# A two-layer graph network on one core: a new opening of set-up, and a fixed place for each load of A

## The chip, the cores and the metric

The kernel runs on one core of one Trainium2 chip. The metric is the device time of one execution in microseconds (us), as the median of several runs. A core has five engines that matter here: TensorE (PE in the profile, with PEld for its weight loads), VectorE (DVE), ScalarE (ACT), GpSimd (POOL) and SyncE (SP). SP, ACT and POOL also issue the DMA transfers that this text speaks of. Each engine takes its own instructions in their order.

## The reference

The input is x (4096 x 512) and a symmetric 0/1 adjacency matrix A (4096 x 4096). Two layers follow each other, each with a residual and a layer norm. Cut to what matters:

```python
# layer 0: graph attention with 8 heads of 64
feats = einsum('nf,hfo->hno', x, W)
s_self, s_neigh = einsum(feats, a_self), einsum(feats, a_neigh)    # one number per head and node
dense = leaky_relu(s_self[:, :, None] + s_neigh[:, None, :], 0.2) * A
out = softmax(dense) @ feats + b
x = layernorm(x + relu(out))
# layer 1: attention inside 32 graphs of 128 nodes, with A added to the scores
q, k, v = x @ Wq.T + bq, x @ Wk.T + bk, x @ Wv.T + bv
scores = (where(mask, q @ k.T * scale, 0) + 2 * A) * where(mask, 1, -1e6)
x = layernorm(x + (softmax(scores) * mask) @ v)
```

## The kernel before

**Stages.** Set-up (0 to about 160 us) makes the features of layer 0 and all that depends on one node alone. Four passes follow, one for each pair of heads r = 0 to 3. A pass goes over four chunks c of 1024 target nodes, and in each chunk over the 32 tiles j of 128 source nodes, eight at a time in passes 0 to 2 and four at a time in pass 3. Pass 0 also turns A: it loads A, transposes it, and stores the result in DRAM (`at_d`), from which passes 1 to 3 read. Layer 1 runs inside and after pass 3.

**Who orders the work.** PE's instructions stand in the order in which the program writes them. For the other engines and for DMA issues a scheduler chooses the order, except for an instruction that is given to `tc.keep_in_program_order`. A tile pool with n buffers makes the n+1st tile wait until the first is no longer used.

**Set-up.** x is treated in eight blocks k of four tiles u of 128 rows. For each block:

- `load_rows(k)` loads four x tiles (`xt_f`, pool of four). Block 0 is issued on SP, the others on ACT.
- `turn_rows(k)` transposes them on PE, 16 transposes (L650), into four PSUM tiles `ps_set` (pool of three; in block 0 the last goes to a `ps_m` bank), one for each 128 columns c of x. ACT copies each to SBUF as `xT_f` (L653), and sums it on the way into `xs`.
- `features(k, u)` multiplies a tile with W (`w_sb_f`) into `ps_fe` (L722, pool of two): eight instructions, which the profile records as sixteen. W has two more columns a head, W a_self and W a_neigh, so that the scores come out with the features. In block 0 the first three tiles go without them (256 columns in place of 264), and `first_scores` (L746) makes up for them.
- DVE adds b (L733), which frees the `ps_fe` buffer; `exponentials` make the factors that depend on one node (`e_all`, `pu_j`, `d_all`).
- `scaled_features(k, u)` makes what the passes multiply with: ACT writes `fst` (L775), DVE writes a second part of `fst` (L776) and `gst` (L766), and POOL stores both to DRAM as `f_d` and `g_d`.
- `rows_of_exponentials(k)` stores rows of factors, `pu_d`, one block later.

The two score columns of W are made at the start on DVE: for each of the four chunks c of W two multiplies (L634) and two reductions (L635), with a_self and a_neigh spread over all partitions in one `fst` buffer (the pool has three). The transposes of block k+1 stand behind the first product of block k, except for block 1, whose transposes stand behind the third product of block 0.

**Loads of A.** `load_adjacency(c, j)` issues on POOL a load of 1024 x 512 elements of A (`a_b`, converted to 8 bits, pool of three). Such a block holds four tiles j. The first three are issued in set-up; every other is issued by `bring(0, c, j)` at the tile that needs it, and the scheduler moves it up. `bring` transposes two tiles of A at once on PE (L1130), ACT casts them to `at` (L1134, twelve buffers in passes 0 to 2), and POOL stores them (`at_d`, L1135).

**One step of pass 0.** For eight tiles j: DVE makes sixteen `q` (L1386, eight buffers), ACT and DVE the marks (L1395, L1391); PE computes `accf` (L1406, from `at` and `f_s`), transposes A for four coming tiles, computes `acc` (L1426, from `q` and `g_s`), `dens` (L1441, from the marks) and `ae` (L1350, from `at`), and transposes A for four more. SP loads `f_s` and `g_s` (two buffers each) for every four tiles, and `p_row` (two buffers) and `u_row` (one) for every chunk c.

Of the kernel before, what the change touches and what calls it, by code (L numbers as in the profile page):

```python
# [10 lines left out]
F32 = mybir.dt.float32  # L11
# [393 lines left out]
def adjacency_streamed_path(  # L405
# [159 lines left out]
    def sums_to_columns(dst, part):  # L565

        for m in range(FC):
            nc.tensor.matmul(
                dst[:, m : m + 1], part[:, ts(m, P)], pick_col, start=True, stop=True
            )  # L570

    ats = {}
    a_bs = {}
# [12 lines left out]
    with tc.tile_pool(name="setup1", bufs=1, side="right") as one, tc.tile_pool(  # L586
# [28 lines left out]
        a_b2 = staged.tile([P, PR, 2, 2, FP], F32R, name="fst").bitcast(F32)  # L615
        a_b2 = a_b2[:, :2].rearrange("p r u s n -> p (r u s n)").rearrange(
            "p (k h o) -> p k h o", k=2, h=H
        )
        for k, v in enumerate((a_self, a_neigh)):
            nc.sync.dma_start(  # L620
                a_b2[:, k].rearrange("p h o -> p (h o)"), broadcast_rows(v, P, H * FH)
            )
# [7 lines left out]
        load_rows(1)  # L630
        for c in range(FC):
            prod = qp.tile([P, C], F32, name="q").rearrange("p (k h o) -> p k h o", k=2, h=H)
            for k in range(2):
                nc.vector.tensor_mul(prod[:, k], w_sb[:, c, :, :FH], a_b2[:, k])  # L634
                nc.vector.tensor_reduce(w_sb[:, c, :, FH + k], prod[:, k], AX.X, OP.add)  # L635
# [3 lines left out]
        xs = one.tile([P, FC, NB], F32, name="xs")  # L639

        def turn_rows(k):
            xT = xTs[k] = two.tile([P, FC, 4, P], F32, name="xT_f")
            pts = {}

            order = [(u, c) for u in range(4) for c in range(FC)]
            for u, c in order if k == 0 else sorted(order, key=lambda x: x[1]):
                if u == 0:
                    last = k == 0 and c == FC - 1
                    pts[c] = misc([P, 4, P]) if last else pss.tile([P, 4, P], F32, name="ps_set")
                nc.tensor.transpose(pts[c][:, u, :], xts[k][u][:, ts(c, P)], ident)  # L650
            for c in range(FC):
                pt = pts[c]
                nc.scalar.activation(  # L653
                    xT[:, c], pt, AF.Identity, accum_out=xs[:, c, k : k + 1]
                )
# [59 lines left out]
        def features(k, u):  # L715
            pf = psf.tile([P, 2, HB], F32, name="ps_fe")
            pf = pf[:, :, : H * FW // 2].rearrange("p q (h w) -> p q h w", w=FW)
            scored = k > 0 or u == 3
            cols = slice(0, FW if scored else FH)
            for c in range(FC):  # L720
                for q in range(2):
                    nc.tensor.matmul(  # L722
                        pf[:, q, :, cols],
                        tile_j(xTs[k][:, c].rearrange("p u n -> p (u n)"), u),
                        w_sb[:, c, 4 * q : 4 * q + 4, cols],
                        start=(c == 0),
                        stop=(c == FC - 1),
                    )
# [12 lines left out]
        def first_scores():  # L741

            ps = pss.tile([P, 4, H, 2], F32, name="ps_set")
            for u in range(3):
                for c in range(FC):
# [7 lines left out]
                    )  # L753
            for u in range(3):
                exponentials(0, u, ps[:, u].rearrange("p (q h) w -> p q h w", q=2))

        def scaled_features(k, u):
            j, v, i = 4 * k + u, u // 2, u % 2
            fb = sums[k, v][:, i]
            if i == 0:  # L760
# [14 lines left out]
            nc.scalar.activation(fst[:, :, i, 0, :], fr, AF.Copy, scale=-1.0)  # L775
            nc.vector.scalar_tensor_tensor(  # L776
                fst[:, :, i, 1, :],
# [4 lines left out]
                op1=OP.subtract,  # L782
            )
            if i:
                for dst, n, src in (
# [330 lines left out]
    def bring(r, c, j):  # L1116
# [12 lines left out]
        for t in range(CT):  # L1129
            nc.tensor.transpose(pt[:, t, :], pairs[:, t, :], ident_b)  # L1130
        both = pt.rearrange("p t n -> p (t n)").bitcast(FP8).rearrange("p (n k) -> p n k", k=2)
        for k in range(2):
# [192 lines left out]
    def main_pass(r, ae=None, wide=4):  # L1325

        for c in range(NCH):
            p_row = []
            for h in range(2):
                p_row.append(rowp.tile([P, C], F32, name=f"p_row{h}"))  # L1330
                nc.sync.dma_start(p_row[h], broadcast_rows(pu_d[2 * r + h, ts(c, C)], P, C))
            u_row = urowp.tile([P, C], F32, name="u_row")
            for h in range(2):
                nc.sync.dma_start(
                    u_row[h * FH : (h + 1) * FH, :],
                    broadcast_rows(pu_d[H + 2 * r + h, ts(c, C)], FH, C),
                )
# [23 lines left out]
            for j0 in range(0, NT, wide):  # L1361
# [3 lines left out]
                for k in range(j0 // 4, (j0 + wide) // 4):  # L1365
                    f_s[k] = fsp.tile([P, 4, 2, FP], F32R, name="f_s")
                    nc.sync.dma_start(
                        f_s[k].rearrange("p u s n -> p (u s n)").bitcast(F32), f_d[r, k]
                    )
                    g_s[k] = gfp.tile([P, 4, 2, FH], F32, name="g_s")  # L1370
                    nc.sync.dma_start(g_s[k].rearrange("p u h o -> p (u h o)"), g_d[r, k])
                if at_step == 0:
# [178 lines left out]
```

## Time and profile before

| | |
|---|---|
| median of three runs | 2067.01 us (2066.73 to 2069.36) |
| the profiled execution | 2068.04 us, of which the profile's span is 2066.2 us |
| PE busy | 2030.9 us, 98% of the span |
| DVE, ACT, POOL busy | 81%, 75%, 11% |
| set-up, from the first instruction to the first transpose of A | 159.8 us |
| PE's first transpose, PE's first product L722 | 3.91 us, 13.93 us |
| mean share of the DMA engines, 60 to 120 us and 120 to 620 us | 1.04, 1.03 |

The profile is of one execution. Its span runs from the first to the last instruction of the core; the execution's own time has 1.8 us around it. The granted clock of PE is given as a share of full speed. A wait is put down to the work that ended last ahead of it.

### The profile page before, as it was taken

The numbers are of one execution on the slowest core, as the hardware profiler recorded it, in microseconds if no ns is written. First come the engines' busy times: TensorE is split into PE (matmuls) and PEld (weight loads), VectorE is DVE, ScalarE is ACT, GpSimd is POOL, SyncE is SP. The second block draws the span as 40 slices with busy tenths as digits, with TensorE's granted clock in tenths as the row PEclk, the third lists the DMA queues.
The fourth block names the chain that finished last, engine by engine and source line by source line (L and its number), as shares of the span: only waits on it lengthen the run. The fifth ranks groups of instructions, "written<-read, shape, count | busy, mean of one in ns | idle before, by whom it ended". The sixth has DMA issues, their size and how long they took to land.

```text
span 2066.2 us, 38253 instructions
## 1 busy us (share of the span) xinstructions
PE 2030.9 (98%) x15086; PEld 1049.8 (51%) x15086; DVE 1670.1 (81%) x2125; ACT 1540.4 (75%) x1869; POOL 222.9 (11%) x361
## 2 busy tenths in 40 slices
PE   8999999999999999999999999999999999999997
PEld 6885555444445444444445444444454445445443
DVE  5667888888799998798999899998975884896654
ACT  3338888888878899788899899998885666567420
POOL 1223222222100000000000000000210210210111
PEclk9999999999999999999999999999999999999999
DMA  6989999999899999798999899989974773684211
GB/s 195 303 270 248 270 294 263 296 260 297 264 341 335 367 347 350 258 312 293 327 308 338 300 354 329 329 287 360 315 247 150 240 262 128 229 275 167 74 49 43
DMA packets 207371, 551.31 MB, mean 267 GB/s; under 512 B 24780, under 2 KB 65740, under 8 KB 207180
## 3 DMA queue, kind: packets, MB, share of 16 engines
q1 hardware_dynamic: 136716, 418.45, 58.1%
q0 software_dynamic: 62272, 121.91, 23.1%
q10 hardware_dynamic: 8192, 8.39, 1.2%
q8 instruction: 121, 1.98, 0.4%
q14 instruction: 70, 0.57, 0.1%
HBM read 491.79 MB, written 107.22 MB: 290 GB/s over the span
## 4 chain that ended last, share of the span: by engine, by line
PE 84%; DMA 7%; issue 4%; DVE 2%; ACT 1%; POOL 1%; POOLq 0%; ACTq 0%; DVEq 0%; SPq 0%
PE acc L1426 36%; PE accf L1406 20%; PE ps_m L1067 5%; PE ps_fe L722 5%; PE ps_m L995 5%; DMA at_d<-at 5%; PE dens L1441 5%; PE ps_m L1022 1%; DVE q L1386 1%; PE ps_m L1081 1%; DMA xt_f<-in_x_dram 1%; ACT mark L1395 1%; PE ps_m L975 1%; PE ps_m L1130 1%; PE ps_m L924 1%
## 5 line engine op out<-in xcount | busy, mean ns | idle before, releaser
L1386 DVE SCALAR_TENSOR_TENSOR q<-p_row,d_all,at 128x1024 f32<-128x1024 f32 x1024 | 1241.9, 1277 | 159.9 <-PE acc L1426 129.3
L1395 ACT ACTIVATE mark<-q,nb_all 128x1024 fp8e4<-128x1024 f32 x896 | 995.5, 1145 | 181.4 <-DVE q L1386 165.8
L1426 PE MATMUL acc<-q,g_s 128*32 128x512 f32 x8192 | 904.2, 593 | 1.4 <-DVE q L1386 0.4
L1426 PEld LDWEIGHTS acc<-q,g_s 128*32 128x32 f32 x8192 | 264.3, 110 | 595.3 <-issue 533.6
L1406 PE MATMUL accf<-at,f_s 128*128 128x512 f32 x2048 | 496.7, 398 | 1.9 <-issue 1.8
L1406 PEld LDWEIGHTS accf<-at,f_s 128*128 128x128 f32 x2048 | 380.5, 189 | 111.4 <-issue 28.1
L1151 ACT ACTIVATE ck<-ck,neg_half_f 128x1024 f32<-128x1024 f32 x128 | 146.0, 1141 | 21.7 <-DMA ck<-in_adj_dram 21.7
L1152 ACT ACTIVATE ck<-ck,neg_quarter 128x1024 f32<-128x1024 f32 x128 | 146.4, 1143 | 1.7
L1441 PE MATMUL dens<-mark,e_b 128*6 128x512 fp8e4 x2048 | 125.9, 379 | 0.9 <-ACT mark L1395 0.9
L722 PE MATMUL ps_fe<-w_sb_f,xT_f 128*128 128x264 f32 (+1 forms) x512 | 121.3, 394 | 4.6 <-ACT xT_f L653 4.6
L1134 ACT CAST at<-ps_m 128x1024 fp32r<-128x1024 fp8e4 x128 | 120.1, 1026 | 5.5 <-ACT mark L1395 3.0
L1067 PE MATMUL ps_m<-wvT,x1T 128*128 128x512 f32 x256 | 114.2, 594 | 0.0
L995 PE MATMUL ps_m<-x1T,M_sb 128*128 128x512 f32 x256 | 112.9, 595 | 0.0
L722 PEld LDWEIGHTS ps_fe<-w_sb_f,xT_f 128*128 128x128 f32 x512 | 100.7, 200 | 19.1 <-ACT xT_f L653 5.0
L1271 POOL DMA_DIRECT2D hs_d<-hst x12 | 10.7, 893 | 834.4 <-DVE hst L1261 816.1
L1391 DVE TENSOR_SCALAR mark<-q,d_all 128x1024 fp8e4<-128x1024 f32 x128 | 95.7, 748 | 4.8
L1441 PEld LDWEIGHTS <-e_b 128*6 128x6 bf16 x2048 | 55.8, 86 | 78.5 <-issue 36.2
L1135 POOL DMA_DIRECT2D at_d<-at x128 | 69.0, 539 | 178.0 <-ACT at L1134 107.4
L995 PEld LDWEIGHTS ps_m<-x1T,M_sb 128*128 128x128 f32 x256 | 48.0, 190 | 59.3 <-issue 58.4
L1067 PEld LDWEIGHTS ps_m<-wvT,x1T 128*128 128x128 f32 x256 | 47.6, 190 | 56.4 <-issue 55.1
L1075 DVE TENSOR_TENSOR v_t<-ps_m,bv_row 128x512 f32<-128x512 f32 x32 | 21.7, 683 | 60.5 <-PE ps_m L1067 60.5
L1002 ACT ACTIVATE zT<-ps_m,zb 128x512 f32<-128x512 f32 x32 | 21.8, 680 | 61.1 <-PE ps_m L995 61.1
(185 smaller groups left out, 1084.2 us busy)
## 6 DMA issues: line engine op xcount, KB each, us to landing
at<-at_d SPq DMA_DIRECT2D x384, 512.0 KB, 6.0
f_s<-f_d SPq DMA_DIRECT2D x128, 512.0 KB, 7.5
at_d<-at POOLq DMA_DIRECT2D x128, 512.0 KB, 14.9
ck<-in_adj_dram SPq DMA_DIRECT2D x128, 512.0 KB, 5.4
g_s<-g_d SPq DMA_DIRECT2D x128, 256.0 KB, 5.7
f_d<-fst POOLq DMA_DIRECT2D x16, 1024.0 KB, 7.2
a_b<-in_adj_dram POOLq DMA_DIRECT2D x32, 512.0 KB, 16.3
p_row<-pu_d SPq DMA_DIRECT2D x32, 512.0 KB, 6.7
```

Of the source, the lines that this page charges most:

```text
L722: nc.tensor.matmul(pf[:, q, :, cols], tile_j(xTs[k][:, c].rearrange("p u n -> p (u n)"), u), w_sb[:, c, 4 * q : 4 * q + 4, cols], start=(c ...
L995: nc.tensor.matmul(pz, L1["M"][:, f, ts(c, P)], x1T[:, f, :], start=(f == 0), stop=(f == FC - 1),)
L1067: nc.tensor.matmul(pv, x1T[:, f, ts(u, P)], L1["wvT"][:, f, :], start=(f == 0), stop=(f == FC - 1),)
L1134: nc.scalar.copy(at, both[:, :, k])
L1151: tc.keep_in_program_order(nc.scalar.activation(ck, ck, AF.Square, bias=neg_half))
L1152: nc.scalar.activation(ck, ck, AF.Abs, bias=neg_quarter, accum_out=binp[:, k : k + 1])
L1386: nc.vector.scalar_tensor_tensor(q, p_row[h], d_j, ats[r, c, j].bitcast(F32), op0=OP.max, op1=OP.mult)
L1391: nc.vector.tensor_scalar(mark, q, d_j, None, op0=OP.is_gt, saturate=False)
L1395: nc.scalar.activation(mark, q, AF.Sigmoid, bias=nb_all[:, j, hh : hh + 1], scale=BIG, saturate=False,)
L1406: nc.tensor.matmul(accf[:, s, :], f_s[j // 4][:, j % 4, w, :], ats[r, c, j][:, ts(s, HB)], start=(j == 0 and w == 0), stop=(j == NT - 1 an ...
L1426: nc.tensor.matmul(acc[o : o + 32, s, :], g_s[j // 4][:, j % 4, h, o % FH : o % FH + 32], qs[j, h][:, ts(s, HB)], start=(j == 0), stop=(j ...
L1441: nc.tensor.matmul(dens[lo : lo + 6, :], e_b[:, j, 2 * r + h, :], marks[j, h][:, ts(s, HB)], start=(j == 0), stop=(j == NT - 1),)
```

## The change

It has two parts.

In set-up, SP issues the first two x tiles, then the second half of W, a_self, a_neigh (now in an `fst` buffer each), the other two x tiles, b, and all later x tiles; ACT issues only the first half of W, and then runs a one-column activation at once. Block 0 is turned in two halves: two tiles are transposed and copied, the product of tile 0 and the first half of that of tile 1 follow, then the other two tiles are transposed. Ahead of the first and of the second x tile PE transposes the unit matrix, nine times and twice (`keep_warm`), into a `ps_fe` buffer that no one reads. None of block 0's four tiles takes its scores with its features now; `first_scores` covers all four and comes behind tile 3, as do block 1's transposes. The score columns of W's second half are made behind the first two products. Several instructions are pinned to the program's order.

In pass 0, `bring` issues the load of the block three places up right behind the transposes of a block's second half. The loads of `p_row` and `u_row` of the first two chunks and of `f_s` and `g_s` of the first sixteen tiles are pinned.

```diff
+    def in_order(pinned, ins):
+        if pinned:
+            tc.keep_in_program_order(ins)
...
-        def load_rows(k):
-            xts[k] = []
-            for u in range(4):
+        def load_rows(k, us=range(4)):
+            xts.setdefault(k, [])
+            for u in us:
                 xt = xtp.tile([P, F], F32, name="xt_f")
-                queue = nc.scalar if k else nc.sync
-                queue.dma_start(xt, x[ts(4 * k + u, P), :])
+                nc.sync.dma_start(xt, x[ts(4 * k + u, P), :])
...
-        load_rows(0)
+        load_rows(0, (0, 1))
...
-            nc.scalar.dma_start(
+            queue = nc.scalar if c < FC // 2 else nc.sync
+            queue.dma_start(
                 w_sb[:, c, :, :FH], W[:, ts(c, P), :].rearrange("h p o -> p h o")
             )
...
+        nc.scalar.activation(neg_quarter, neg_quarter, AF.Identity)
...
+            nc.sync.dma_start(a_s[k], broadcast_rows(v, P, H * FH))
+        load_rows(0, (2, 3))
         b_row = one.tile([P, H * FH], F32, name="b_row")
         nc.sync.dma_start(b_row, broadcast_rows(b, P, H * FH))
+        load_rows(1)
...
+        def score_columns(c, pinned=True):
...
+        for c in range(FC // 2):
+            score_columns(c, False)
...
+            def keep_warm(n):
+                pw = psf.tile([P, 2, HB], F32, name="ps_fe")
+                for i in range(n):
+                    nc.tensor.transpose(pw[:, 0, :P], ident, ident)
+
+            order = [(u, c) for u in us for c in range(FC)]
             for u, c in order if k == 0 else sorted(order, key=lambda x: x[1]):
...
+                if (k, c) == (0, 0) and u < 2:
+                    keep_warm((9, 2)[u])
+                nc.tensor.transpose(turned[c][:, u, :], xts[k][u][:, ts(c, P)], ident)
...
-            scored = k > 0 or u == 3
+            scored = k > 0
...
+                if (k, u, c) == (0, 1, 1):
+                    turn_rows(0, (2, 3))
...
-            for u in range(3):
+            for u in range(4):
                 for c in range(FC):
                     nc.tensor.matmul(
                         ps[:, u],
...
-        turn_rows(0)
+        turn_rows(0, (0, 1))
         for k in range(NB):
             for u in range(4):
                 features(k, u)
-                if u == (0 if k else 2) and k + 1 < NB:
+                if k == 0 and u < 2:
+                    score_columns(FC // 2 + u)
+                if u == (0 if k else 3) and k + 1 < NB:
                     turn_rows(k + 1)
...
-                if u == 2 and k == 0:
+                if u == 3 and k == 0:
                     first_scores()
...
+        ahead = c * NT + j + 10
+        if j % 4 == 2 and ahead < NCH * NT:
+            tc.keep_in_program_order(load_adjacency(ahead // NT, ahead % NT))
...
+                in_order(
+                    r == 0 and c < 2,
+                    nc.sync.dma_start(p_row[h], broadcast_rows(pu_d[2 * r + h, ts(c, C)], P, C)),
+                )
...
+                    in_order(r == 0 and c == 0 and j0 < 16, ins)
```

In the changed kernel L650 becomes L674, L653 becomes L677, L722 becomes L749, L733 becomes L762, L775 becomes L804, L634 and L635 become L638 and L642, L746 becomes L775, and L1130 becomes L1162.

More of the change, by code (lines that the diff above doesn't have):

```diff
@@ L611, in adjacency_streamed_path @@
         for c in range(FC):
-            nc.scalar.dma_start(
+            queue = nc.scalar if c < FC // 2 else nc.sync
+            queue.dma_start(
                 w_sb[:, c, :, :FH], W[:, ts(c, P), :].rearrange("h p o -> p h o")
             )
[L615 to L618, printed above, removed]
+        nc.scalar.activation(neg_quarter, neg_quarter, AF.Identity)
+        a_s = [staged.tile([P, PR, 2, 2, FP], F32R, name="fst").bitcast(F32) for _ in range(2)]
+        a_s = [a.rearrange("p r u s n -> p (r u s n)")[:, : H * FH] for a in a_s]
         for k, v in enumerate((a_self, a_neigh)):
-            nc.sync.dma_start(
-                a_b2[:, k].rearrange("p h o -> p (h o)"), broadcast_rows(v, P, H * FH)
-            )
+            nc.sync.dma_start(a_s[k], broadcast_rows(v, P, H * FH))
+        load_rows(0, (2, 3))
         b_row = one.tile([P, H * FH], F32, name="b_row")
         nc.sync.dma_start(b_row, broadcast_rows(b, P, H * FH))
+        load_rows(1)
         b_col = one.tile([P, PR], F32, name="b_col")
@@ L629, in adjacency_streamed_path @@
         )
-        load_rows(1)
-        for c in range(FC):
+        def score_columns(c, pinned=True):
             prod = qp.tile([P, C], F32, name="q").rearrange("p (k h o) -> p k h o", k=2, h=H)
             for k in range(2):
-                nc.vector.tensor_mul(prod[:, k], w_sb[:, c, :, :FH], a_b2[:, k])
-                nc.vector.tensor_reduce(w_sb[:, c, :, FH + k], prod[:, k], AX.X, OP.add)
+                ins = nc.vector.tensor_mul(
+                    prod[:, k], w_sb[:, c, :, :FH], a_s[k].rearrange("p (h o) -> p h o", h=H)
+                )
+                in_order(pinned, ins)
+                ins = nc.vector.tensor_reduce(
+                    w_sb[:, c, :, FH + k], prod[:, k], AX.X, OP.add
+                )
+                in_order(pinned, ins)
+        for c in range(FC // 2):
+            score_columns(c, False)
         powers = one.tile([P, 5, H], F32, name="powers")
@@ L638, in adjacency_streamed_path, with turn_rows @@
             nc.vector.memset(powers[:, i, :], v)
[L639 to L645, printed above, removed]
+        xs = one.tile([P, FC, NB + 1], F32, name="xs")
+        turned = {}
+        def turn_rows(k, us=range(4)):
+            if us[0] == 0:
+                xTs[k] = two.tile([P, FC, 4, P], F32, name="xT_f")
+                turned.clear()
+            xT, n = xTs[k], slice(us[0], us[-1] + 1)
+            for c in range(FC):
+                if us[0] == 0:
+                    last = k == 0 and c == FC - 1
+                    turned[c] = misc([P, 4, P]) if last else pss.tile([P, 4, P], F32, name="ps_set")
+            def keep_warm(n):
[3 more added lines that the diff above has]
+            order = [(u, c) for u in us for c in range(FC)]
             for u, c in order if k == 0 else sorted(order, key=lambda x: x[1]):
[L647 to L650, printed above, removed]
+                if (k, c) == (0, 0) and u < 2:
+                    keep_warm((9, 2)[u])
+                nc.tensor.transpose(turned[c][:, u, :], xts[k][u][:, ts(c, P)], ident)
+            at = NB if us[0] else k
             for c in range(FC):
-                pt = pts[c]
                 nc.scalar.activation(
-                    xT[:, c], pt, AF.Identity, accum_out=xs[:, c, k : k + 1]
+                    xT[:, c, n],
+                    turned[c][:, n],
+                    AF.Identity,
+                    accum_out=xs[:, c, at : at + 1],
                 )
@@ L753, in first_scores @@
                     )
-            for u in range(3):
+            for u in range(4):
                 exponentials(0, u, ps[:, u].rearrange("p (q h) w -> p q h w", q=2))
@@ L775, in scaled_features @@
             nc.scalar.activation(fst[:, :, i, 0, :], fr, AF.Copy, scale=-1.0)
-            nc.vector.scalar_tensor_tensor(
+            ins = nc.vector.scalar_tensor_tensor(
                 fst[:, :, i, 1, :],
@@ L783, in scaled_features @@
             )
+            in_order(k == 0, ins)
             if i:
@@ L1330, in main_pass @@
                 p_row.append(rowp.tile([P, C], F32, name=f"p_row{h}"))
-                nc.sync.dma_start(p_row[h], broadcast_rows(pu_d[2 * r + h, ts(c, C)], P, C))
+                in_order(
+                    r == 0 and c < 2,
+                    nc.sync.dma_start(p_row[h], broadcast_rows(pu_d[2 * r + h, ts(c, C)], P, C)),
+                )
             u_row = urowp.tile([P, C], F32, name="u_row")
             for h in range(2):
-                nc.sync.dma_start(
-                    u_row[h * FH : (h + 1) * FH, :],
-                    broadcast_rows(pu_d[H + 2 * r + h, ts(c, C)], FH, C),
+                in_order(
+                    r == 0 and c < 2,
+                    nc.sync.dma_start(
+                        u_row[h * FH : (h + 1) * FH, :],
+                        broadcast_rows(pu_d[H + 2 * r + h, ts(c, C)], FH, C),
+                    ),
                 )
@@ L1366, in main_pass @@
                     f_s[k] = fsp.tile([P, 4, 2, FP], F32R, name="f_s")
-                    nc.sync.dma_start(
+                    ins = nc.sync.dma_start(
                         f_s[k].rearrange("p u s n -> p (u s n)").bitcast(F32), f_d[r, k]
                     )
+                    in_order(r == 0 and c == 0 and j0 < 16, ins)
                     g_s[k] = gfp.tile([P, 4, 2, FH], F32, name="g_s")
-                    nc.sync.dma_start(g_s[k].rearrange("p u h o -> p (u h o)"), g_d[r, k])
+                    ins = nc.sync.dma_start(
+                        g_s[k].rearrange("p u h o -> p (u h o)"), g_d[r, k]
+                    )
+                    in_order(r == 0 and c == 0 and j0 < 16, ins)
                 if at_step == 0:
```

## The prediction

> **What bounds the kernel now.** I read the page's part 1 first, then the list of what TensorE (PE) waited for, then the chain of waits over the first 45 us, then the table by stretches. The page says who is full:
>
> ```profile
> PE 2030.9 (98%) x15086; PEld 1049.8 (51%) x15086; DVE 1670.1 (81%) x2125; ACT 1540.4 (75%) x1869; POOL 222.9 (11%) x361
> PE   8999999999999999999999999999999999999997
> ```
>
> PE is busy in 2030.9 of 2066.2 us; only the first and last slices fall below 9. So a change can gain PE's idle time where it acts, PE work done at a low clock, or PE instructions that it removes. The idle time, from PE's waits:
>
> ```profile
> PE ps_set L650 <- DMA xt_f<-in_x_dram: 6.4, 4, 3.9
> PE ps_fe L722 <- ACT xT_f L653: 4.6, 1, 4.6
> PE ps_m L1130 <- ACT at L1134: 2.0, 2, 1.2
> PE ps_set L695 <- ACT pu_j L671: 1.3, 1, 1.3
> PE dens L1441 <- ACT mark L1395: 0.9, 2, 0.7
> ```
>
> (engine, waiting line, releaser: us, times, longest.) The first two, 11.0 us, lie in set-up: 9.8 at the opening and 1.24 at 92.7 us, where block 5's x came late. The other three lie at the end of set-up and in pass 0. No transpose of A (L1130) waits for its load. The opening, as the chain (start, us, what):
>
> ```profile
> 0.73 3.05 DMA xt_f<-in_x_dram
> 3.78 0.02 issue
> 3.80 8.09 DMA w_sb_f<-in_L_gnn_W_dram
> 11.89 0.00 issue
> 11.89 1.28 ACT L653
> 13.17 0.01 issue
> 13.19 0.70 ACT xT_f L653 x2
> 13.88 0.04 issue
> 13.93 12.03 PE ps_fe L722 x48
> 25.95 1.87 PE ps_set L650 x16
> 27.83 3.06 PE ps_set L746 x24
> 30.88 8.75 PE ps_fe L722 x32
> 39.63 1.93 PE ps_set L650 x16
> ```
>
> PE had all of block 0's transposes done by 9.3 us. ACT, which must copy them out, was still issuing: four loads of W, then four of block 1's x at 7.39 to 11.86, each behind an earlier transfer. Then it loaded its table (1.28), and the first product started at 13.93. The landmark is 39.63, block 2's transposes: before and after, the same products precede it and from there the two PE orders agree.
>
> **What the Trainium skill says.** "TensorE: Matmul & The Clock Gate", Part 1, says that PE's clock is halved by default, and that free-running windows of about 3.4 us decide. The trace agrees: these stretches (PE busy, clock, DMA share, GB/s) hold scores, then dense products, half speed, then full again.
>
> ```profile
> 27.05:30.46 3.41, 3.41 (x29) 1.00 0.98 316
> 30.46:33.87 3.41, 3.41 (x10) 0.50 0.67 237
> 33.87:37.28 3.41, 3.41 (x17) 1.00 0.01 2
> ```
>
> "ScalarE: Activation LUTs", What ACT_TABLE_LOAD costs, gives 1283 ns; here 1.28 us. "DMA: Bandwidth & Descriptors", Issuing engines are not separate DMA queues: a second issuing engine saves issue time alone, so moving x from ACT to SP adds no bandwidth; what it can free is ACT. The same page's Specifications want 512 bytes a piece for full rate; W's pieces are 256 bytes (4096 packets for 1 MB), so I count W double.
>
> **The change, part by part.**
>
> *Opening loads.* SP now issues x tiles 0, 1, W chunks 2, 3, a_self, a_neigh, x 2, 3, b, x of block 1; ACT issues W 0, 1 and loads its table near 3 us. x 1 should land as before, 5.7. W's first landing took 6.3 us after issue, so W 0 at 7.0 to 7.4. PE's first product therefore starts at 7.2 instead of 13.93: 6.7 earlier. ACT's first half-copy, near 6.5, is not last there.
>
> *What is late next.* DVE. Before, a_self landed at 9.07 behind 1 MB of x and part of W; now it is behind 0.5 MB of x and most of W. Counted double where it is W, that is 2.75 MB against about 2.4 at some 0.37 MB/us: 10.2. From there DVE works 8 multiplies and reduces for W 0, 1 (8 x 0.64 = 5.1), a small cast (0.2), and the bias add L762 (0.7): 16.2. In the built order ACT has the scaled copy L804 of tile 0 *ahead of* the copies of x tiles 2 and 3, so those wait for DVE: 16.3 + 0.63 + 0.5 = 17.5. Tile 2's product starts there. PE's own path comes close: tile 0 from 7.2 (cold until about 10, then 2.1) to 12.1; half of tile 1, 1.7; 8 transposes, 0.9 (x 2 and 3 are issued once W 0 has landed, whose semaphore they share in the built program, so they land near 7.2 + 5.1 = 12.3, in time); the other half, 1.7: 16.5. So PE idles 1.0, and half of what the early start wins is given to DVE.
>
> *From there to the landmark.* Warm rates are 223 ns per 264-column record (3.57 for 16), scaled to 216 for 256 columns; scores 122 ns. Tiles 2 and 3: 2 x 3.46. Transposes of block 1: 1.9. Scores, now for four tiles: 32 x 0.122 = 3.9 (8 records more than the 24, +1.0, less 0.1 for a narrower tile 3). Tile (1,0): 3.57. A cold window after the scores, as before: 3.4 us at half, 1.7. Sum 17.5 + 6.92 + 1.9 + 3.9 + 3.57 + 1.7 = 35.5. Gain 39.63 - 35.5 = **4.1**.
>
> *Unit transposes.* 11 x 0.21 cold = 2.3 us of PE, issued from 1.5 us on while PE has no data. Cover: the wait for x 0 (3.88) and x 1 (5.7). Without it they cost up to 2.3. Their gain is at most the cold loss before 10 us, 1.4; behind DVE it is worth 0. I take 0, range -0.5 to +1.4.
>
> *x on SP; p_row, u_row, f_s, g_s behind it.* In 60 to 95 us, p_row and u_row landings took 12.7 to 13.8 us and x up to 11.7; block 5's x was 1.24 late. In the new SP order all 28 x loads precede them, so they go out at about 106 to 115, still 35 us ahead of pass 0. I take the 1.24 as gained; bounds 0 (congestion stays, the shares at 60 to 110 being 1.04 and more) and 1.24. f_s/g_s of cycle 0 have the same cover. Removing 28 issues of about 0.35 to 1.3 us from ACT is worth nothing more: PE bounds that stage.
>
> *Pinned SP order in pass 0.* With T for the first accf product (165.2): cycle 1's second f_s now stands behind a g_s that waits until T + 18 and is needed at T + 32; f_s lands in 8. p_row of c = 1 moves from 107 into pass 0, at T + 78, needed at T + 100; longest p_row landing 12.7. Cost 0 while these hold.
>
> *Loads of A.* The load three blocks up already followed its buffer's release. Blocks 3 and 4 now go out at about T - 2 and T instead of T + 6 and T + 17; no one waited for them, gain 0. In the steady part the load moves behind two stores at_d on POOL:
>
> ```profile
> 194.24 0.90 POOL L581 DMA_DIRECT2D a_b<-in_adj_dram  x1 [2.84 <-PE ps_m L1130]
> 197.42 0.55 POOL L1135 DMA_DIRECT2D at_d<-at  x1 [2.29 <-ACT at L1134]
> 198.34 0.53 POOL L1135 DMA_DIRECT2D at_d<-at  x1 [0.36 <-ACT at L1134]
> ```
>
> So it leaves at 198.9 instead of 194.2. Its block is transposed at 226.96: lead 28 against a longest landing of 23.7. Cost 0. Queued behind the waiting load are the next at_d stores; the buffers they free are held by the ae products until 192 and later anyway.
>
> *ACT order in cycle 0.* Four casts now precede seven marks. DVE's q, one per 1.2 us, paces those marks to about 188.5 either way, before dens at 189.75: 0.
>
> **Sum.** 4.1 + 1.24 = 5.4; against the profiled execution's 2068.04 (span 2066.2, 1.84 around it) that is 2062.6. That execution is 1.03 above the median 2067.01, so for the median **2061.6**. A difference under 0.2%, 4.1 us, I count as no change.
>
> **Rivals.** (a) *DVE is not last.* a_self lands at 9.1, the unit transposes keep PE warm from 7.2 on: tile 2 starts near 15.8, and the second cold window is missed. Landmark 32.8 to 33.8, gain 5.8 to 6.8 plus 1.24, in the middle 7.6: 2059.4. For: PE can run tile 0 as soon as W 0 lands at 7.2, and a warm clock takes 1.4 off its path. Against: DVE has 6.0 us of work between a_self and the copies, whatever PE does.
> (b) *The half-block hurts itself.* W, doubled in weight, delays a_self or b to 12, ACT's queued copy holds tile 2 until 19, and x of block 5 stays late: gain 2.5 to 3.5, 2064. For: the four W landings took 9.1 in the median. The change then doesn't do in full what its early start promises.
> (c) *Slower: the load of A comes late on POOL.* Decides when an a_b landing exceeds the 28 us left. DMA shares of 1.10 to 1.15 in pass 0 speak for it; no landing over 23.7 speaks against it. At 29 each of some 14 blocks with this short lead (every second one) costs 1 us; less the 5.4 that is +8.6, 2075.6.
> The clock at the set-up's end adds noise to all: 0.50 from 160.2 to 170.4, and where the windows fall after the shift is open, 3.4 x 0.5 / 2 = +-0.9.
>
> **How the numbers follow.** Forecast 0.57, (a) 0.17, (b) 0.19, (c) 0.07. The forecast's own bounds are 3.9 to 6.5, a little of it below 4.1. Faster: 0.55 + 0.17; same: 0.02 + 0.18; slower: 0.07 + 0.01. Range 2058.4 (a, warm, with the clock's luck) to 2065.2 (b, x late); outside are (c) and the far ends.
>
> **What would show it.** Right: first L749 product near 7.2; a PE gap of about 1 us ahead of tile 2's product, released by ACT; block 2's transposes near 35.5; no x wait at 88; set-up ends 5 us earlier and every pass as long as before. Wrong: PE waits for a_b or p_row in pass 0, a landmark above 37 or below 33.5, or passes 1 to 3 of another length.

## The result: 5 us slower, with the opening as forecast

| | before | after |
|---|---|---|
| median | 2067.7 us (14 runs) | 2072.7 us (14 runs) |
| profiled execution, its span | 2068.04, 2066.2 | 2072.73, 2070.8 |
| first product of set-up | 13.93 | 6.84 |
| block 2's transposes (the landmark) | 39.63 | 35.42 |
| first transpose of A | 159.8 | 154.1 |
| first `accf` product of pass 0 | 165.16 | 159.36 |
| first `accf` product of pass 1 | 592.31 | 598.32 |

The ratio after to before is 1.0024, with a 95% interval from 1.0016 to 1.0032: slower, where the forecast was 5.4 us faster. Pass 0 begins 5.8 us earlier and ends 6.0 us later.

First the part that came as forecast. The chain of waits over the first 40 us of the changed kernel (start, us, what):

```profile
2.74 3.78 SPq L624
6.53 0.04 issue
6.57 5.11 DMA fst<-in_L_gnn_a_neigh_dram
...
15.42 0.69 DVE q L762
16.11 0.02 issue
16.13 0.63 ACT fst L804
16.76 0.37 ACT xT_f L677 x2
17.13 0.04 issue
17.18 7.18 PE ps_fe L749 x32
24.36 1.87 PE ps_set L674 x16
26.23 4.04 PE ps_set L775 x32
30.27 5.15 PE ps_fe L749 x16
35.42 1.93 PE ps_set L674 x16
```

The path is no longer x, W and ACT's table, as before, but a_self and a_neigh, DVE, and ACT's scaled copy L804 that stands ahead of the half-block's copies. (SPq is SP issuing a transfer: the issue of a_self alone took 3.78 us, so a_neigh went out only at 6.57.) The forecast had 17.5 for tile 2's product and 35.5 for the landmark.

Then the part that did not. The list of what PE waited for over the whole execution:

```profile
PE dens L1486 <- ACT mark L1440: 6.6, 10, 0.7
...
PE ps_fe L668 <- POOL ident_f masks.py:199: 1.4, 1, 1.4
...
PE ps_fe L749 <- ACT xT_f L677: 1.1, 1, 1.1
```

Before, `dens` waited 0.9 us in 2 for the marks; now 6.6 us in 10. The waits for x are down from 6.4 us to 0.6. The shares of the chain that ended last (part 4 of the page) say the same in another way: DMA held 7% of that chain before, and now

```profile
PE 82%; DMA 10%; issue 4%; DVE 2%; ACT 1%; POOL 1%; SPq 0%; POOLq 0%; DVEq 0%
```

To place the loss, PE's timeline was cut at the starts of the `accf` products of pass 0. From one such start to the next is a cycle, the work on eight tiles; pass 0 has sixteen, four to a chunk. Cycle 0 is 1.2 us shorter than before, two cycles are longer, and the others are the same within 0.4:

| first cycle of | before | after |
|---|---|---|
| chunk 2 | 377.38 to 404.41: 27.0 us | 370.40 to 404.62: 34.2 us |
| chunk 3 | 485.26 to 511.45: 26.2 us | 485.31 to 517.85: 32.5 us |

Together they lose 13.5 us. The head start gave 5.8, cycle 0 gave 1.2 and the other cycles 0.5, so pass 1 starts 6.0 later. Passes 1 and 2 are as long as before; the spans differ by 4.6 in the end, so 1.4 came back late in the kernel, and why is open. Inside the first of the two long cycles, PE's timeline (start, us, engine, line, what):

```profile
370.40 7.60 PE L1451 MATMUL accf<-at,f_s 128*128 128x512 f32 x32
377.85 1.07 PE L1162 MATMUL ps_m<-ident_b,a_b 128*128 128x128 bf16 x16
378.84 10.51 PE L1471 MATMUL acc<-q,g_s 128*32 128x512 f32 x96
389.56 5.07 PE L1471 MATMUL acc<-q,g_s 128*32 128x512 f32 x30 [0.21 <-DVE q L1431]
...
397.08 0.38 PE L1486 MATMUL dens<-mark,e_b 128*6 128x512 fp8e4 x1 [0.65 <-ACT mark L1440]
398.11 0.39 PE L1486 MATMUL dens<-mark,e_b 128*6 128x512 fp8e4 x3 [0.66 <-ACT mark L1440]
...
401.44 1.60 PE L1391 MATMUL ae<-at,e_p 128*25 128x512 bf16 x16
402.97 1.89 PE L1162 MATMUL ps_m<-ident_b,a_b 128*128 128x128 bf16 x16
```

PE is not stopped, it is paced: each `dens` comes 1.04 us after the one before, when ACT has written the next mark. And ACT's timeline of the same cycle:

```profile
372.50 3.74 ACT L1169 CAST at<-ps_m 128x1024 fp32r<-128x1024 fp8e4 x4
386.56 0.59 ACT L1230 COPY hst<-ae 128x512 f32<-128x512 f32 x1 [10.32 <-DMA hs_d<-hst]
387.04 3.23 ACT L1440 ACTIVATE mark<-q,nb_all 128x1024 fp8e4<-128x1024 f32 x3
```

ACT stood still for 10.3 us. At the end of a chunk, `sums_to_rows` copies `ae` out of PSUM into `aes`, which takes the tile `hst` of a pool with one buffer. The chunk before has stored its rows from that same tile (`hs_d`, on POOL's queue), and the store was issued only at 369.32 and landed at 386.5. The marks that the cycle still lacked, and four casts `at`, stand behind this copy on ACT. DVE feels it too: ACT's marks read the `q`, so with ACT standing the eight `q` buffers stay taken. The kernel before has no such row among DVE's waits of pass 0:

```profile
DVE q L1431 <- ACT mark L1440: 6.8, 4, 2.5
```

So the first of the two cycles loses its 7.2 us in three ways: 2.3 in `acc`, whose `q` come late; 3.6 in `dens`, which follow ACT's marks; and 1.3 in the `ae` products and the transposes behind them, which take 1.60 and 1.89 us instead of 1.09 and 1.07. From 402 to 404 us the granted clock was 0.50, where the kernel before had 1.00; just ahead of that, from 396 to 400, PE was busy in only 0.76 of every 2 us.

The wait of ACT's copy stood in the kernel before as well, but shorter:

```profile
387.62 0.59 ACT L1195 COPY hst<-ae 128x512 f32<-128x512 f32 x1 [4.41 <-DMA hs_d<-hst]
494.68 0.59 ACT L1195 COPY hst<-ae 128x512 f32<-128x512 f32 x1 [3.58 <-DMA hs_d<-hst]
```

In the kernel before, the two stores took 11.3 and 10.5 us from issue to landing; in the changed kernel 17.2 and 15.3. No transpose of A waits for its load in pass 0: the longest `a_b` landing is 25.2 us of the 28 that the prediction counted.

### The profile page after: what moved, and what is told of

Read it like the earlier page. It is cut to its first block, busy times and chain, and to the rows that moved or that the text cites. A ratio compares the mean times of both kernels' runs of the same rounds, so it can differ in the third digit from the quotient of the medians.

```text
span 2070.8 us, 38332 instructions
## 1 busy us (share of the span) xinstructions
PE 2037.8 (98%) x15105; PEld 1052.9 (51%) x15105; DVE 1671.5 (81%) x2125; ACT 1540.0 (74%) x1878; POOL 224.6 (11%) x361
## 4 chain that ended last, share of the span: by engine, by line
PE 82%; DMA 10%; issue 4%; DVE 2%; ACT 1%; POOL 1%; SPq 0%; POOLq 0%; DVEq 0%
PE acc L1471 35%; PE accf L1451 20%; PE ps_m L1099 5%; PE ps_fe L749 5%; PE ps_m L1027 5%; DMA at_d<-at 5%; PE dens L1486 5%; DMA a_b<-in_adj_dram 4%; PE ps_m L1054 1%; DVE q L1431 1%; PE ps_m L1113 1%; PE ps_m L1007 1%; PE ps_m L956 1%; PE ps_set L674 1%; PE ps_m L1162 1%
## 5 line engine op out<-in xcount | busy, mean ns | idle before, releaser
L749 PE MATMUL ps_fe<-w_sb_f,xT_f 128*128 128x264 f32 (+1 forms) x512 | 121.4, 394 | 1.1 <-ACT xT_f L677 1.1
L749 PEld LDWEIGHTS ps_fe<-w_sb_f,xT_f 128*128 128x128 f32 x512 | 100.4, 200 | 15.7 <-ACT xT_f L677 1.8
## 6 DMA issues: line engine op xcount, KB each, us to landing
at_d<-at POOLq DMA_DIRECT2D x128, 512.0 KB, 15.7
a_b<-in_adj_dram POOLq DMA_DIRECT2D x32, 512.0 KB, 18.8
```

Of the source, the lines that this page charges most:

```text
L749: nc.tensor.matmul(pf[:, q, :, cols], tile_j(xTs[k][:, c].rearrange("p u n -> p (u n)"), u), w_sb[:, c, 4 * q : 4 * q + 4, cols], start=(c ...
```

## The experiments

Three theories stood: (1) the load of A, pinned behind two stores, changes when POOL's queue is full, and `hs_d` lands later for it; (2) pass 0 is held by DMA traffic, so that any head start of PE is lost at a chunk's end; (3) the backlog itself, or what the pinned SP order added to it, holds PE. "First cycles" below are those of chunks 2 and 3, and the landings are those of their `hs_d`. Times are from each kernel's trace, medians and ratios (with 95% interval) from its runs. A ratio is to the runs of the kernel before that were taken alongside (medians 2066.3 to 2067.7), so rows are best compared by their ratios. A trace is of one execution; those of e6, e8, e9 and e14 lie more than 3 us from their kernels' medians (e6's 6.3), so there trace and median can differ in what they show.

| kernel | median, us | ratio | first cycles, us | `hs_d` landings, us |
|---|---|---|---|---|
| before | 2067.7 | | 27.0, 26.2 | 11.3, 10.5 |
| after | 2072.7 | 1.0024 (1.0016 to 1.0032) | 34.2, 32.5 | 17.2, 15.3 |
| e1 before + load edit | 2075.2 | 1.0039 (1.0026 to 1.0052) | 33.6, 31.4 | 16.6, 14.7 |
| e2 after, own `aes` | 2058.0 | 0.9955 (0.9943 to 0.9968) | 25.8, 25.8 | 16.9, 15.7 |
| e3 after, loads first | 2064.5 | 0.9987 (0.9978 to 0.9995) | 32.1, 27.2 | 15.4, 11.4 |
| e4 before, own `aes` | 2063.8 | 0.9986 (0.9979 to 0.9993) | 25.8, 25.8 | 12.2, 11.0 |
| e13 e3, `p_row` in set-up | 2060.1 | 0.9965 (0.9951 to 0.9979) | 27.8, 25.8 | 12.1, 10.0 |
| e14 before, `p_row` in pass 0 | 2069.7 | 1.0016 (1.0010 to 1.0023) | 28.6, 25.8 | 12.9, 9.6 |

**e1: the load edit alone.**

```diff
+        ahead = c * NT + j + 10          # the kernel before, plus this
+        if j % 4 == 2 and ahead < NCH * NT:
+            tc.keep_in_program_order(load_adjacency(ahead // NT, ahead % NT))
```

> The kernel before, with one part of the change alone: the load of A's block three places up is pinned behind the stores of the second half-block, in pass 0. Theory 1 (the order on POOL): the load leaves some 4 us later, the DMA queue runs partly empty and then carries a backlog at each end of a chunk; the store hs_d lands 15 to 17 us after issue instead of 10.5 to 11.3, ACT's copy of ae waits for it 8 to 10 us instead of 3.6 to 4.4, TensorE waits for the marks (dens, about 0.65 us each time) and the first cycle of chunks 2 and 3 takes some 5 to 7 us longer each: 8 to 14 us slower than before, 2076 to 2082. Theory 2 (pass 0 is held by the amount of DMA traffic, and a head start from set-up is simply eaten at the next chunk end): there is no head start here, so no loss in the cycle from about 377 to 404 us; within 2 us of before, at most 6 slower from the cycle at 485 us, which theory 2 does not explain.

2075.2 us, 8 slower than before, with no head start; that is just under the expected range. Its waits in pass 0 (PE's, then ACT's):

```profile
PE dens L1444 <- ACT mark L1398: 6.5, 10, 0.7
```

```profile
ACT hst L1198 <- DMA hs_d<-hst: 17.5, 2, 9.7
```

The load edit alone brings both long cycles, so theory 1 holds, and theory 2 alone can't be the cause. What the edit does to the queue is seen in POOL's timeline of the changed kernel:

```profile
190.16 0.53 POOL L1170 DMA_DIRECT2D at_d<-at  x1 [10.33 <-ACT at L1169]
191.08 0.53 POOL L1170 DMA_DIRECT2D at_d<-at  x1 [0.38 <-ACT at L1169]
191.60 1.05 POOL L586 DMA_DIRECT2D a_b<-in_adj_dram  x1
192.64 1.07 POOL L1170 DMA_DIRECT2D at_d<-at  x2
199.20 0.53 POOL L1170 DMA_DIRECT2D at_d<-at  x1 [5.49 <-DMA a_b<-in_adj_dram]
```

The load waits with the stores for ACT's casts, and then five transfers of 0.5 MB go out in 3.5 us. In between the queue runs low. These stretches of the kernel before and then of the changed one lie at the same place in the work, since both began a cycle at 485.3 (us of PE, PEld, DVE, ACT and POOL, then clock, DMA share, GB/s):

```profile
460.00:464.00 4.00, 4.00 (x19) 3.27 (x18) 3.47 (x6) 4.00 (x6) 1.62 (x3) 1.00 1.07 124
464.00:468.00 4.00, 4.00 (x37) 2.55 (x39) 0.00 (x0) 3.44 (x4) 1.41 (x2) 1.00 1.15 133
```

```profile
460.00:464.00 4.00, 4.00 (x19) 3.24 (x19) 3.52 (x6) 4.00 (x6) 2.25 (x3) 1.00 0.68 244
464.00:468.00 4.00, 4.00 (x37) 2.61 (x39) 0.00 (x0) 3.43 (x4) 1.39 (x4) 1.00 0.95 271
```

The share is 0.68 and 0.95 instead of 1.07 and 1.15, in a pass where it is 1.1 on the average up to the first `hs_d`. (It counts time; the bytes moved in these stretches are more, 244 and 271 GB/s, so the mix of transfers differs too.) The time left unused comes to 2.4 us, and it is missing at 484, when `hs_d` joins the queue. That is half of the 4.8 us by which this store lands later; the rest isn't shown. Ahead of the other long cycle the changed kernel has no such gap: from 230 to 370 us no stretch of 4 us falls below 1.02. That the order of load and stores is the cause rests on e1 and e3, not on this picture.

**e2 and e4: the copy gets a buffer of its own**, in the changed kernel and in the one before.

```diff
-            aes = hp_.tile([P, CT, FP], F32, name="hst")
-            aes = aes.rearrange("p t n -> p (t n)")[:, :HB]
+            if c < NCH - 1:
+                aes = pools["aes"].tile([P, HB], F32, name="aes")   # a new pool of one buffer
+            else:
...
```

> The changed kernel, where the copy of ae (aes) of chunks 0 to 2 has a buffer of its own instead of taking the tile hst that the store hs_d still reads. Both theories 1 and 2 say that the wait of ACT for hs_d is what TensorE pays for: the waits of dens for the marks (6.6 us in 10) and the two long first cycles (34.2 and 32.5 us instead of 27.0 and 26.2) go, though hs_d still takes 15 to 17 us to land: 13 us off the changed kernel, 2059 to 2061, which is faster than before by 7. Rival (theory 3: the backlog itself, late f_s, g_s, p_row and A loads, holds TensorE, and the wait for hs_d is only a sign of it): under 4 us is gained, 2069 or more, and other waits stand in those cycles.

> The kernel before with a buffer of its own for aes of chunks 0 to 2. Its ACT waited 8.0 us in two for hs_d, and TensorE only 0.9 us for the marks. All theories: 0.5 to 1.5 us faster than before, 2066.2 to 2067.2; it tells what of a gain in the changed kernel with that buffer is the wait that the change brought, and what the kernel before already had.

e2 ran in 2058.0, 14.7 less than the changed kernel (14.2 by the ratios), although `hs_d` still took 16.9 and 15.7 us to land. So the late store matters through this one copy and not otherwise, and the first form of theory 3, a backlog that holds PE by itself, falls. ACT's copy, and the shares of the chain that ended last, in e2:

```profile
372.06 0.58 ACT L1233 COPY aes<-ae 128x512 f32<-128x512 f32 x1
```

```profile
PE 94%; DVE 3%; issue 1%; DMA 0%; ACT 0%; SPq 0%; POOL 0%; POOLq 0%; DVEq 0%
```

DMA has left the chain. e4 gained 3.0 us on the kernel before, more than the expected 1.5: the wait cost it not only the 0.9 us of `dens`; its two first cycles shrank by 1.2 and 0.4 and the two cycles behind them by 0.4 each. The two kernels with this buffer differ by 5.8 us: that is what the change is worth where the store can't hold ACT.

**e3: the load ahead of the stores.**

```diff
-            nc.gpsimd.dma_start(at_d[c, j + k], at.bitcast(F32))
+            stores.append((c, j + k, at))
+        if j % 4 == 2:                      # behind the pinned load
+            for c_, j_, at in stores:
+                nc.gpsimd.dma_start(at_d[c_, j_], at.bitcast(F32))
+            stores.clear()
```

> The changed kernel, where the two stores of the second half-block are put behind the load on POOL instead of ahead of it: the load leaves first, then four stores together. Theory 1: the load leaves about 4 us earlier, hs_d lands in 10 to 12 us again, ACT waits about 4 us for it, dens waits under 2 us in all, and both long cycles are back at 26 to 27 us: 2060 to 2063. Theory 2: the amount of traffic is the same and TensorE is 7 us ahead at 370 us, so the first long cycle stays at about 34 us and only the second shortens: 2066 to 2067. If neither cycle shortens (2071 to 2073), the order of load and stores is not the cause.

2064.5. The cycle of chunk 3 was mended, 27.2 us with `hs_d` landing in 11.4, as theory 1 has it; that of chunk 2 was not, 32.1 us, as theory 2 has it. Something else delays the first store:

```profile
382.67 0.58 ACT L1236 COPY hst<-ae 128x512 f32<-128x512 f32 x1 [8.47 <-DMA hs_d<-hst]
```

**e5, e7, e8: parts that should cost nothing once the wait is gone.** All three have the buffer of its own. e5 adds e3's order, e7 leaves out `keep_warm` (its two lines in `turn_rows`), e8 leaves out the load edit.

> The changed kernel with both: the buffer of its own for aes (as in the second experiment) and the load of A ahead of the second half-block's stores (as in the third). If the wait for hs_d was the only thing that either order cost, then with the wait gone the order is worth nothing: 2056 to 2060, as with the buffer alone (2058.0), no TensorE wait for marks, all first cycles at 25.8 us. If loads that leave 4 us earlier are worth something in themselves, 2054 or less; if it is above 2061, the order of POOL costs by another way.

> The changed kernel with the buffer of its own for aes, and without the 11 unit-matrix transposes of the opening. The prediction took them as worth 0 (bounds: without them 1.4 slower to 0.5 faster): 2058.0 within 1, TensorE at half speed until about 10 us, block 2's transposes between 34 and 37 us. Rival (they keep the clock up, so tile 0 runs at full speed): the product of tile 0 takes 2 us longer without them, 2060 or more.

> The changed kernel with the buffer of its own for aes, and with the load edit undone (the builder then puts two loads behind the first eight stores, and later each load ahead of four stores). The prediction took the load edit as worth 0 but for the wait that was found since: 2056 to 2060, passes as long as in the second experiment. Rival: the edit brings loads forward at the start of pass 0, and without it transposes of A wait for their loads there: cycles 0 and 1 are 2 to 6 us longer, 2060 to 2064.

2058.7 (0.9955, 0.9943 to 0.9966), 2057.3 (0.9955, 0.9942 to 0.9968) and 2058.5 (0.9948, 0.9936 to 0.9961): not to be told from e2 or from each other. In all of them the first cycles last 25.8 us. So neither the place of the load nor the unit transposes is worth more than these intervals leave, about 2.5 us either way. The traces narrow it for the unit transposes: without them tile 2's product starts at 17.55, with them at 17.18 (the changed kernel) and 17.05 (e2).

**e6: `hs_d` of pass 0 on SP's queue.**

```diff
-                nc.gpsimd.dma_start(
+                (nc.gpsimd if r else nc.sync).dma_start(
                     hs_d[ts(c, C), ts(r, FP)].rearrange("(t p) n -> p t n", p=P), hst
```

> The changed kernel with pass 0's stores hs_d issued on SP instead of POOL; aes still shares the tile. Stores and A loads on POOL's queue took 15 to 25 us to land in this stretch, f_s and g_s on SP's queue 6 to 8. If hs_d is late because it stands behind POOL's own backlog: it lands in 6 to 9 us, ACT waits under 3 us, dens waits under 1 us, first cycles at 26 to 27 us: 2058 to 2060. Rival: the 16 DMA engines are full, so a store is late on any queue: landing 12 us or more, and the first cycles stay over 30 us: 2066 or more.

2068.4 (1.0011, 1.0004 to 1.0018), better than the changed kernel but no cure. Its trace is of an execution of 2062.1 us, the fastest of 22, so most of them lost more than it shows. `hs_d` took 13.1 and 14.3 us on this queue too, and the first cycles lasted 28.6 and 31.4. SP had issued two `p_row` of 0.5 MB some 6 us ahead of the first; those landed in 7.5 us in the median. Why the store takes nearly twice as long as loads of its size on that queue is open.

**e9 to e12: the parts without the pins, and without the load edit.** e9 is e3 and e12 is e2, each with the order on SP no longer pinned; e10 is the changed kernel without the load edit; e11 is e10 without the pins too, so that the opening is left alone. In all but e12 the copy shares the tile.

```diff
-                    r == 0 and c < 2,
+                    False and c < 2,
...
-                    in_order(r == 0 and c == 0 and j0 < 16, ins)
+                    in_order(False and c == 0 and j0 < 16, ins)
```

> The third experiment's kernel (loads first, aes in the shared tile) without the order pinned on SP, so that p_row of the second chunk goes out in set-up again, as in the kernel before. The third experiment mended the second long cycle (27.2 us) but not the first (32.1): from the first accf product to hs_d its trace has six p_row transfers, the kernel before four. Theory 3 (the two p_row loads moved into pass 0, 1 MB or some 3.6 us of a full DMA, are that backlog): the first cycle is at 27 to 28.5 us, hs_d lands in under 12.5 us: 2060 to 2062, unless x comes late in set-up. Theory 2 (TensorE's head start alone meets a DMA stream that has not gained it): the first cycle stays at 31 to 33 us, 2064 to 2066.

> The changed kernel with the load edit alone undone, aes in the shared tile. Its second long cycle should be mended as in the third experiment (26 to 27.5 us); the first stays long by theories 2 and 3 alike (30 to 33 us): 2063 to 2066. If both cycles are at 27 us or less, the load edit was the whole of the loss: 2059 to 2061.

> The opening alone: the load edit and the order pinned on SP are both undone, so POOL's order of loads and stores is that of the kernel before. Theory 3: no extra p_row in pass 0, first cycle 27 to 28.5 us, second 26 to 27: 2060 to 2063. Theory 2: the head start of 5.8 us is eaten at the first chunk end whatever the order: first cycle 31 to 33 us, 2065 to 2067, as if nothing had been changed.

> The changed kernel with the buffer of its own for aes and without the order pinned on SP. With the wait for hs_d gone the pins are worth nothing in pass 0; in set-up SP's f_s and p_row loads may stand ahead of x again: 2057 to 2060 if x still comes in time, up to 2062 if TensorE waits for x as it did before (1.2 us at 92.7) or longer.

e9 ran in 2065.4 (0.9995, 0.9986 to 1.0003), e11 in 2066.4 (0.9997, 0.9989 to 1.0005), e12 in 2064.1 (0.9983, 0.9975 to 0.9991), where at most 2062 was expected. None could answer the question on the first cycle (29.3 us in e9, 27.5 in e11), because the head start was gone before pass 0. What PE waited for in set-up, in e11:

```profile
PE ps_set L674 <- DMA xt_f<-in_x_dram: 5.1, 6, 1.9
PE ps_fe L668 <- POOL ident_f masks.py:199: 1.4, 1, 1.4
PE ps_fe L749 <- ACT xT_f L677: 0.5, 1, 0.5
```

Without pins SP's `p_row` and `f_s` loads stand ahead of x; PE waits 5.1 us for x between 85 and 93, and its clock falls to half between 88 and 98. So moving x to SP needs the pins: e12, whose PE waits 5.4 us for x, is 6.1 us slower than e2.

e10 ran in 2065.7 (0.9994, 0.9986 to 1.0003). Its first cycles are 27.6 and 25.8, where 30 to 33 was expected of the first. But its cycle 0 took 31.1 instead of 27.4: here the scheduler put twelve stores and then four loads, and PE did wait for A. At chunk 2 PE was only 1.7 us ahead of the kernel before.

```profile
PE ps_m L1162 <- DMA a_b<-in_adj_dram: 3.2, 1, 3.2
```

In e8, where the same edit is undone with the extra buffer, the first loads stand behind eight stores, and there is no such wait.

**e13 and e14: where `p_row` of chunk 1 is loaded.** From the first `accf` product to the first `hs_d`, the trace of e3 has six `p_row` transfers and that of the kernel before four. The pins had moved two, 1 MB, from set-up into pass 0. e13 is e3 with these two issued right behind the first chunk's rows, all else in the same order; e14 is the kernel before with the two pinned into pass 0.

```diff
+            if (r, c) == (0, 0):          # e13: the loads of chunk 1, ahead of f_s and g_s
+                p_row_1 = load_p_row(1)
...
+                if r == 0 and c == 1:     # e14: in the kernel before
+                    tc.keep_in_program_order(ins)
```

> The third experiment's kernel (the whole change, loads first, aes in the shared tile) with the two p_row loads of the second chunk issued in set-up, directly behind the first chunk's rows, and everything else in the same order on SP and POOL. x stays first on SP, so the head start of TensorE stays. Theory 3 (the 1 MB of p_row in pass 0 is the backlog): first cycle of chunk 2 at 27 to 28.5 us instead of 32.1, hs_d lands in under 12 us: 2059 to 2062. Theory 2 (the head start alone meets the full DMA): first cycle 31 to 33 us, hs_d 14 us or more: 2064 to 2066.

> The kernel before with the two p_row loads of the second chunk pinned into pass 0, behind cycle 1's f_s and g_s, and nothing else changed. No head start, loads and stores on POOL as before. Theory 3: hs_d lands in 14 us or more, first cycle of chunk 2 at 30 to 32 us instead of 27.0, 3 to 5 us slower than before: 2070 to 2072. Theory 2: first cycle at 27 to 27.5 us, 2066 to 2068.

e13 ran in 2060.1: with the same head start the first cycle is 27.8 instead of 32.1, and against e3 the ratio falls from 0.9987 to 0.9965, 4.5 us. That is theory 3's second form. It refutes theory 2 in the form that any head start is lost: the first `accf` product came at 159.42, 5.7 us ahead of the kernel before, and pass 1 began 6.3 us ahead of it. The two cycles alone would prove less, since the traced execution of e3 began pass 0 at 157.35, 2.1 us earlier still; the medians carry it. ACT's copy:

```profile
381.75 0.59 ACT L1236 COPY hst<-ae 128x512 f32<-128x512 f32 x1 [5.18 <-DMA hs_d<-hst]
```

e14 was slower by 3.4 us (2069.7, expected 2070 to 2072), with its first cycle at 28.6: the sign of theory 3, but less of it than the expected 30 to 32. Its profiled execution, 2066.2 us, lies 3.5 below its own median, so the trace probably shows less than the runs had. In e10 too the megabyte lay in pass 0, and with PE hardly ahead the first cycle was 27.6. So the megabyte may weigh more where PE is ahead, and what is left of theory 2 is not excluded. How a load issued at 233 us (e3) still delays a store issued at 367 isn't shown step by step either; between the two the DMA share was at least 1.03 in every 4 us.

The kernels with the shared tile agree: at landings of 9.6 to 10 us the cycle has its free length, 25.8; at 11.3 it is 27.0, at 12.1 27.8, at 13.1 28.6, at 14.7 31.4, at 17.2 34.2. Up to 13.1 us each us of a late store costs about 1 us of PE, over the whole range 1.2. The longer cycles add the low clock behind the paced `dens`, 0.9 to 1.6 us; it stands in e9's trace too, the row that fits worst (12.5 us, 29.3).

## Why the prediction was wrong, step by step

**Opening loads, "What is late next", the landmark: right.** First product 6.84 (forecast 7.2); a_self landed at 10.06 (10.2, though the figures given, 0.35 MB more at 0.37 MB/us behind 9.07, make it 10.0); DVE's L762 ended at 16.1 (16.2); tile 2's product at 17.18 (17.5), with a gap of 1.1 us put down to ACT (1.0); landmark 35.42 (35.5). The cold window behind the scores came, as the stretches show that answer to those of before:

```profile
27.05:30.46 3.41, 3.41 (x27) 3.41 (x27) 0.15 (x2) 0.72 (x3) 0.00 (x0) 0.90 0.87 298
30.46:33.87 3.41, 3.41 (x10) 2.71 (x10) 3.41 (x13) 1.46 (x12) 0.68 (x1) 0.60 0.01 2
33.87:37.28 3.41, 3.41 (x24) 2.97 (x24) 3.41 (x14) 1.33 (x5) 2.75 (x4) 1.00 0.71 250
```

That the landmark fell so near the forecast is in part luck of the clock: with the same opening it came at 33.24 in e3's traced execution and at 36.77 in e2's (the last section), although tile 2's product started at 16.83 and 17.05.

**Unit transposes, 0: not contradicted.** e7 could not tell 0 from the 1.4 that the prediction allowed; tile 2's product started within 0.5 us with and without them.

**x on SP, 1.24: right in size, with a condition that the prediction only half saw.** The wait at 92.7 is gone, and set-up gained 5.7 us where the landmark gained 4.2, so 1.5 behind it, the clock's part included. But the pins carry that: without them it is 5.1 us and a cold clock.

**ACT order in cycle 0, 0: a little more.** Cycle 0 is 1.2 us shorter; its `accf` stretch at the low clock lasts 9.2 us instead of 10.0, the rest was not taken apart.

**"Pinned SP order in pass 0 ... Cost 0 while these hold": the first failed step.** It asked of each moved load only whether its own reader gets it in time, and that was right: no one waited for `p_row`. It did not ask what 1 MB more, in a pass whose DMA share is 1.1, puts off. It put off `hs_d`: e13 against e3, 4.5 us, with the loads first and PE ahead.

**"Loads of A ... Cost 0": the second failed step, and the larger.** The load did leave late as forecast: at 191.60, where the old order, 7.0 us earlier by now, would have had 187.2, so 4.4 us late (forecast 4.7), and its block wasn't late. "Queued behind the waiting load are the next at_d stores; the buffers they free are held by ae products until 192 and later anyway" names the stores and forgets the one transfer on that queue whose buffer someone waits for: `hs_d`, whose tile ACT wants to write 7 us after its issue. The row that shows it, `ACT hst L1195 <- DMA hs_d<-hst`, stood in ACT's waits of the kernel before, 12.1 us in three times, 8.0 of them in these two cycles; of waits, the prediction reads only PE's. Alone the step costs 8 us (e1).

The two costs overlap and can't be added: with the load edit alone (e1) the cycle of chunk 2 is 33.6 us, with both 34.2. With both mended (e13: loads first, `p_row` in set-up) the change gains 6.3 us, near the forecast's 5.4; with both in place it loses 5.0; with the wait taken away from both kernels (e2 against e4) it is worth 5.8.

**The rivals.** (a) and (b) speak of the set-up, and neither came. (c) took the right engine and the right sign, but the wrong victim: it looked for a late load of A and priced it at 14 blocks of 1 us; the longest landing stayed below 28, and PE never waited for A. The "Wrong" signs named were a wait of PE for `a_b` or `p_row` in pass 0, a landmark above 37 or below 33.5, or passes 1 to 3 of another length. None of them came in the profiled execution; the loss was pass 0's, by a store.

**Queues.** The Trainium skill, "DMA: Bandwidth & Descriptors", Queues, rings and completion order, says that each DMA engine takes the queues in turn and works through a queue's descriptors in ring order. The changed kernel's trace agrees for the loads: `at_d` and `a_b` on POOL's queue took 15.3 and 18.8 us to land in the median of 200 to 580 us, `f_s` and `g_s` on SP's 6.7 and 6.1. The store `hs_d` on SP's queue took 13.1 and 14.3 (e6), which taking turns alone doesn't explain.

## What to carry to other kernels

When transfers are moved on a full queue, ask not only when the moved transfer is needed, but which later transfer on that queue has someone waiting for its landing; a store counts as one if its tile is written again. Look for that in the waits of every engine, not only of the busiest: a wait of 4 us that PE hardly feels may be the last slack, and here each further us cost PE 1 to 1.2. A tile of 2 KB a partition with a buffer of its own was worth 3 us to the old kernel and 15 to the new one, more than the change itself.

## What the runs showed of the hardware

- The set-up's length differs between executions with the same opening. By PE's timeline, whose starts are up to 0.2 us ahead of the chain's, the landmark lay at 33.24 (e3), 35.25 (the changed kernel) and 36.77 (e2), where the half clock took none, about one and two of the 3.4 us stretches between 27 and 37 us. The Trainium skill's "TensorE: Matmul & The Clock Gate", Part 1, has these windows run freely, not from the kernel's start; the three numbers fit that, though no run here shows the windows' phase itself. The first `accf` product came at 157.35 (e3), 159.36 and 161.49 (e2).
- PE's busy time rose from 2030.9 to 2037.8 us with nothing added in pass 0 (the unit transposes of set-up are 2.8 of it). Products that show almost no wait but come more slowly (30 `acc` in 5.07 us, 96 in 10.51 just before), and products at half clock, count as busy. Busy time alone doesn't tell work from pace.
- In pass 0 a 0.5 MB load on SP's queue landed in 4.6 to 9.9 us (`f_s`, `p_row`), beside loads of that size on POOL's queue that took 12.7 to 25.2 (`a_b`); a store of that size took 13.1 and 14.3 on SP's queue (e6).
- Behind `dens` paced at one per 1.04 us the granted clock fell to 0.50 (402 to 404 us of the changed kernel), and the `ae` products and transposes there took 1.3 us more. What the pace cost was more than its gaps.
